# A two-layer graph attention on one core: where the exponential of h lies, how the rests of h are turned, and where the last aggregation's scores stand in the order

## The chip, the core and the metric

One core of a Trainium2 chip runs the whole kernel in one launch. The metric is the device time in microseconds (us), and the span is the part of it that the hardware profiler sees. Matmuls run on TensorE (PE; PEld are its weight loads), elementwise work on VectorE (DVE) and ScalarE (ACT), indirect gathers are issued on GpSimd (POOL), and most other transfers on SyncE (SP). Each engine takes its instructions in the order in which they were emitted; engines wait for one another by semaphores. SBUF is the memory on the chip, PSUM the one into which PE writes.

## The reference

3125 nodes with 768 features, 53125 edges (each node has a loop) sorted by target `dst`, three edge types. `x` goes through two layers of relational graph attention, then a residual sum and a layer norm:

```python
def rgat_conv(x, W, q, k, b, src, dst, etype, heads, out_ch, n_nodes):
    xr = jnp.einsum('nd,rdf->rnf', x, W)
    oi, oj = xr[etype, dst], xr[etype, src]
    alpha = jax.nn.leaky_relu(oi @ q + oj @ k, 0.2)
    m = jax.ops.segment_max(alpha, dst, num_segments=n_nodes)
    e = jnp.exp(alpha - m[dst])
    z = jax.ops.segment_sum(e, dst, num_segments=n_nodes)
    a = e / (z[dst] + 1e-16)
    msg = (a[:, :, None] * oj.reshape(-1, heads, out_ch)).reshape(-1, heads * out_ch)
    return jax.ops.segment_sum(msg, dst, num_segments=n_nodes) + b

h = jax.nn.elu(rgat_conv(x, W1, q1, k1, b1, ..., heads=4, out_ch=192))
out = rgat_conv(h, W2, q2, k2, b2, ..., heads=1, out_ch=768)
result = layernorm(x + out)          # over the 768 features, eps 1e-5
```

All inputs and outputs are float32.

## The kernel before, in words

The nodes are cut into `NB` = 25 blocks of 128. The edges of a block are fetched by gathers: each is one indirect DMA (L485, issued on POOL) of 128 rows of a table in device memory, 17 for a block (`SL`; 14 for block 0), 422 in all (`NK`) for each aggregation. The kernel has three stages.

The first (to some 520 us) multiplies x by W1 for the three edge types and stores the rows as the first table (`ftab`).

The second (some 520 to 1131 us, `phase2`, L844) aggregates over the first table and at once multiplies the result by W2, in the same order of blocks. For a block, in two halves of two heads' sums each: the rows are gathered; the scores are put together on DVE (`alpha`, L900 to L907), turned on PE (`turn`, into the PSUM tile `pa`), scanned for the maximum (`scan`, L921 to L926), taken through the exponential on ACT, turned back, and multiplied into selection matrices (`weigh`, L963); PE sums rows with them (`sums`, into `acc`). Then `e_y` (L1011) scales and adds the bias; `e_x` (L1023) takes the exponential on ACT; `e_h` (L1061) makes elu on DVE: L1063 min(ey,1)-1, L1065 for the last 64 of the 192 features of each head (the rests), L1066 for all. h is stored by four DMAs (`h_row`, L1068), and turned by PE (`e_t`, `turned`, L1034) by eight transposes into the two banks of `pt`: four of 128 features and four of the rests. `y` has 256 columns a head for this: 192 and a copy of the last 64. The turned h is split into a high part (`high_parts`: L1044 for the first bank, L1048 twice for the second, ACT) and a low part (`low_parts`: L1055, L1059 twice, DVE), so that products in reduced form add up to float32: `d_products` (L1091) does 72 matmuls a block against W2, in four pieces of 18. `d_row` (L1110) copies a piece's half row out of PSUM on ACT (L1117) and, after a row's second half, stores the whole row (L1119) into the second table. While blocks 15 to 24 are worked on, `move` (L1002 and the line after it) rewrites the table of row numbers piece by piece.

The third (1131 to 1725 us, `phase3`, L1185) gathers from the second table and sums in the same way, but with one head: `a_alpha` (L1305 to L1315), `a_turn`, `a_scan` (L1326 to L1331), `a_exp` (L1335), `a_back`, `weigh` (L1359), `sums` in eight rounds. The rows' own products are added as `r_plus` (L1420), and a product `D` with W2 follows: `d_part` (L1460), one matmul at a time, which the trace shows as two instructions, twelve parts for each block (36 for block 24, which uses W2 split into a high and a low part). That split is made by `w2_high` (L1427, six copies on ACT) and `w2_low` (L1431, six subtractions on DVE) in the buffers of gathers that are done by then. The residual sum and layer norm end a block (L1511 to L1550).

What sets the order is one list for each stage: steps are put down as `when(k, step, block, ...)`, where `k` is a number of slots (one slot per gather), the list is sorted by `k`, and the steps are emitted in that order. `STEPS2` (L89) and `STEPS3` (L103) hold the offsets of the steps from a block's first slot (second stage) or last slot (third). The third stage's scores stand at

```python
"s": (1.9, 3.0, 3.05, 3.1, 5.6, 5.7, 9.5),   # alpha, turn, scan, exp, back, weigh, sums
"d": ((19.5, 22.5, 7), (22.8, 26.2, 5)),      # twelve parts of the product
```

after the block's last slot (slot 422 for block 24), and the parts of the block before fall among them: with a distance of 17, two parts come before the turn and seven before the turn back. For all blocks, once, at the end (L1596):

```python
for t in range(DT):                            # DT = 6, NK = 422
    when(NK + 6 + 0.1 * t, w2_high, t)
    when(NK + 6.01 + 0.1 * t, w2_low, t)
```

Of the kernel before, what the change touches and what calls it, by code (L numbers as in the profile page):

```python
# [9 lines left out]
F32 = mybir.dt.float32  # L10
# [4 lines left out]
AF = mybir.ActivationFunctionType  # L15
ALU = mybir.AluOpType
# [5 lines left out]
P = 128  # L22
# [43 lines left out]
def _index(ap):  # L66
# [22 lines left out]
STEPS2 = {"first": (8.4, 9, 9.05, 11.3, 11.35, 17.4),  # L89
          "second": (16.35, 17.5, 17.55, 19.8, 19.85, 25.9),  # L90
          "f": (-4, 5),
          "marks": 3,
          "h": (26.1, 26.45, 28.4, 28.5, 34.52, 34.6, 34.62),
          "d": ((37, 38.5, 16), (43.2, 45.2, 20), (45.5, 47, 16), (51.7, 53.7, 20)),
          "second0": (13.3, 13.35, 13.4, 13.5, 13.6, 13.65),
          "sums0": (13.45, 13.55),
          "busy": ((0.3, 40), (9.02, 12)),
# [5 lines left out]
STEPS3 = {"f": -13,  # L103
          "marks": -5,
          "q": (-19, -17.27, -3.5, -2),
          "s": (1.9, 3.0, 3.05, 3.1, 5.6, 5.7, 9.5),
          "round": 0.9,
          "r": (16.7, 16.7, 16.72, 16.75, 19.25, 19.3, 16.71, 16.73, 20.5, 20.6),
          "t": (16.74, 16.78),
          "d": ((19.5, 22.5, 7), (22.8, 26.2, 5)),  # L110
          "y": (26.6, 26.7, 26.8, 29.5, 29.6),
# [4 lines left out]
def kernel(  # L116
# [21 lines left out]
    nc = tc.nc  # L138
# [3 lines left out]
    NB = (N + P - 1) // P  # L142
# [4 lines left out]
    H1 = l1["H"]  # L147
    F1 = D // H1
# [4 lines left out]
    HW = RW // 2  # L153
# [6 lines left out]
    V, S, G, T = nc.vector, nc.scalar, nc.gpsimd, Counted(nc.tensor)  # L160
# [14 lines left out]
    ident = keep.tile([P, P], F32, name="fident")  # L175
# [668 lines left out]
    def phase2(work, psum):  # L844
# [9 lines left out]
        rows = [work.tile([P, RW], F32, name=f"r2_{i}", bufs=1) for i in range(WHOLE)]  # L854
# [156 lines left out]
        def e_y(b):  # L1011
            s = blk[b]
            acc = [a[:, :HW].rearrange("p (w f) -> p w f", w=2) for a in s["acc"]]
            rz = work.tile([P, 2, 2], F32, name="rz", bufs=2)
            for c in range(2):
                V.tensor_scalar(rz[:, c], acc[c][:, :, F1], EPS, None, op0=ALU.add)
            V.reciprocal(rz, rz)
            y = s["y"] = work.tile([P, 4, 2 * P], F32, name="y", bufs=1)
            for w in range(4):
                V.scalar_tensor_tensor(y[:, w, :F1], acc[w // 2][:, w % 2, :F1], rz[:, w // 2, w % 2:w % 2 + 1],  # L1020
                                       bias1, op0=ALU.mult, op1=ALU.add)

        def e_x(b):  # L1023
            s = blk[b]
            s["ey"] = work.tile([P, 4, F1], F32, name="ey", bufs=1)
            S.activation(s["ey"], s["y"][:, :, :F1], AF.Exp)

        def busy(n):

# [3 lines left out]

        def turned(s, c):  # L1034

            for t in range(4):
                T.transpose(s["pt"][:, c, t * P:(t + 1) * P], s["y"][:, t, c * P:(c + 1) * P], ident)

        def high_parts(s, c):

            hT = s["hT"].rearrange("p s t (w i) -> p s t w i", i=32)
            pt = s["pt"][:, c].rearrange("p (w h i) -> p h w i", h=H1, i=32)
            if c == 0:
                S.copy(hT[:, 0, :H1], pt)  # L1044
                return
            for u in range(2):
                p = slice(64 * u, 64 * u + 64)
                S.copy(hT[p, 0, H1:], pt[p, u::2])  # L1048

        def low_parts(s, c):  # L1050

            hT = s["hT"].rearrange("p s t (w i) -> p s t w i", i=32)
            pt = s["pt"][:, c].rearrange("p (w h i) -> p h w i", h=H1, i=32)
            if c == 0:
                V.tensor_sub(hT[:, 1, :H1], pt, hT[:, 0, :H1].bitcast(F32))  # L1055
                return
            for u in range(2):
                p = slice(64 * u, 64 * u + 64)
                V.tensor_sub(hT[p, 1, H1:], pt[p, u::2], hT[p, 0, H1:].bitcast(F32))  # L1059

        def e_h(b):  # L1061
            s = blk[b]
            V.tensor_scalar(s["ey"], s["ey"], 1.0, -1.0, op0=ALU.min, op1=ALU.add)  # L1063
            y, ey = s["y"], s["ey"]
            V.scalar_tensor_tensor(y[:, :, F1:], y[:, :, P:F1], 0.0, ey[:, :, P:], op0=ALU.max, op1=ALU.add)  # L1065
            V.scalar_tensor_tensor(y[:, :, :F1], y[:, :, :F1], 0.0, ey, op0=ALU.max, op1=ALU.add)  # L1066

        def h_row(b):  # L1068

            s = blk[b]  # L1070
            s["rows"] = tab2[b * P * R:(b + 1) * P * R, :].rearrange("(n r) f -> n r f", r=R)
            to = s["rows"][:, WHOLE, :D].rearrange("(w i) (h f) -> h i w f", i=32, h=H1)
            for h in range(H1):
                nc.sync.dma_start(to[h], s["y"][32 * h:32 * h + 32, :, :F1])

        def e_t(b):
            s = blk[b]
# [34 lines left out]
        def d_row(b, p):  # L1112
            s = blk[b]
            po = s["po", p]
            r, c = divmod(p, 2)
            n = HW if c == 0 else D + 1 - HW
            S.copy(rows[r][:, c * HW:c * HW + n], po[:, :n])  # L1117
            if c == 1:
                nc.sync.dma_start(s["rows"][:, r, :], rows[r])  # L1119

        def d_tail(b, p):
# [13 lines left out]
        def when(k, f, *a):  # L1135
            ev.append((k, len(ev), f, a))
# [9 lines left out]
        for b in range(NB):  # L1146
            at_0 = base(b + 1) - SL
            when(max(at_0 + STEPS2["marks"], 0.5), marks, b)
            for u, name in enumerate(("first", "second")):
                when(max(at_0 + STEPS2["f"][u], 0.1 + 0.1 * u), f_load, b, u)  # L1150
                for d, f in zip(STEPS2[name], (alpha, turn, scan, back, weigh, sums)):
                    if b > 0:
                        when(at_0 + d, f, b, u)
                if b == 0:
                    for d, f in zip(STEPS2["second0" if u else name], (alpha, turn, scan, back, weigh, sums)):
                        if u == 1 or f is not sums:
                            when(d, f, b, u)
                    if u == 0:
                        for i, d in enumerate(STEPS2["sums0"]):
                            when(d, sums, b, u, i)  # L1160
            for d, f in zip(STEPS2["h"], (e_y, e_x, e_h, h_row, e_t, e_s, e_s2)):
                when(at_0 + d, f, b)
            n = 0
            for i, (a, e, m) in enumerate(STEPS2["d"]):
                for j in range(m):
                    when(at_0 + a + (e - a) * j / m, d_part, b)
                    n += 1
                    for p in range(4):
                        if n == 18 * (p + 1):
                            when(at_0 + a + (e - a) * j / m + STEPS2["copy"], d_row, b, p)  # L1170
                            when(at_0 + a + (e - a) * j / m + STEPS2["tail"], d_tail, b, p)
            assert n == 72
# [431 lines left out]
    with tc.manual_schedule():  # L1604
        with tc.tile_pool(name="share", bufs=1) as pool:
# [5 lines left out]
            with tc.tile_pool(name="wbuf", bufs=1) as wbuf:  # L1611
                weights[0] = [wbuf.tile([P, DT, WA], F32R, name=f"wa{s}") for s in "HL"]
                with tc.tile_pool(name="wrest", bufs=1) as wrest, tc.tile_pool(name="pre", bufs=1) as pre:
# [16 lines left out]
                    with tc.tile_pool(name="work0", bufs=1) as work, tc.tile_pool(  # L1630
                        name="psum0", bufs=1, space=PSUM
# [23 lines left out]
                    with tc.tile_pool(name="work1", bufs=1) as work, tc.tile_pool(  # L1655
                        name="psum1", bufs=1, space=PSUM
# [556 lines left out]
```

## Time and profile before

| | us |
|---|---|
| median of 3 runs | 1728.38 (1726.51 to 1731.38) |
| the profiled execution | 1726.83 |
| its span | 1724.9 |
| PE busy | 1640.5 (95%) |
| DVE busy | 1106.6 (64%) |
| POOL busy | 904.8 (52%) |
| ACT busy | 423.8 (25%) |
| DMA | 500.48 MB, mean 290 GB/s |

The span in 40 equal slices (43 us each); a digit is the busy share in tenths, for PEclk the granted clock of TensorE in tenths of 2.4 GHz:

```profile
PE   9999999999996999999999999939999999999996
POOL 5100000000007777777777777057777777777770
PEclk9999999999997999999999999969999999999999
DMA  9576766666568999999999999569999999999991
```

The two places where PE's digit falls (6 in the thirteenth slice, 3 in the twenty-seventh) are the changes of stage. POOL's digits show where gathers run. A busy share of 7 for POOL does not mean that it has time to spare: an indirect gather of 1.00 us is followed by 0.30 us that the profile counts as idle. The chain of waits follows the work that ended last back through what released it; a group of instructions has its mean duration in ns; a timeline lists the instructions of one engine in order of time.

### The profile page before, as it was taken

The page shows a single profiled execution, that of the slowest core. Times are in us where ns is not written, and L with a number is a line of the kernel's source. Part 1 is how long each engine was busy: PE and PEld are TensorE (multiplying, and loading weights), DVE is VectorE, ACT ScalarE, POOL GpSimd, SP SyncE. Part 2 cuts the span into 40 slices and gives each one's busy share as a digit, 9 for nine tenths or more (in the row PEclk, how much of TensorE's full clock was granted, in tenths as well). Part 3 has the DMA queues.
Part 4 walks back from the last instruction along what each step waited for, and adds up shares of the span by engine and source line. Part 5 has one row for each costly group of instructions (what it writes and reads, how often), then busy time and mean ns, then how long its engine had stood idle before and what let it go on. Part 6 is the DMA issues. An engine that isn't in the chain of part 4 may idle for free.

```text
span 1724.9 us, 39077 instructions
## 1 busy us (share of the span) xinstructions
PE 1640.5 (95%) x14233; PEld 1269.5 (74%) x14233; DVE 1106.6 (64%) x4107; ACT 423.8 (25%) x796; POOL 904.8 (52%) x907
## 2 busy tenths in 40 slices
PE   9999999999996999999999999939999999999996
PEld 8999999999995788888888888924444444444443
DVE  5467666676425566666677777465766666666665
ACT  5122222112110111111111111212333333333333
POOL 5100000000007777777777777057777777777770
PEclk9999999999997999999999999969999999999999
DMA  9576766666568999999999999569999999999991
GB/s 329 180 244 210 258 220 210 199 183 203 191 251 281 330 345 355 347 348 348 346 346 356 354 351 351 172 230 324 334 336 340 335 337 338 338 336 340 334 338 39
DMA packets 169368, 500.48 MB, mean 290 GB/s; under 512 B 39891, under 2 KB 82490, under 8 KB 169167
## 3 DMA queue, kind: packets, MB, share of 16 engines
q0 software_dynamic: 70832, 343.91, 56.1%
q1 hardware_dynamic: 90104, 143.89, 25.0%
q10 hardware_dynamic: 8230, 10.10, 1.7%
q8 instruction: 114, 1.87, 0.4%
q14 instruction: 88, 0.71, 0.1%
HBM read 412.96 MB, written 89.63 MB: 291 GB/s over the span
## 4 chain that ended last, share of the span: by engine, by line
PE 69%; DMA 12%; issue 8%; POOL 6%; DVE 4%; ACT 0%; POOLq 0%; DVEq 0%; ACTq 0%; SPq 0%
PE po L56 47%; PE acc L56 13%; PE D L56 4%; DMA waH<-ftab,ridx 3%; DMA waL<-ftab,ridx 3%; POOL waH L485 2%; PE pa L59 2%; PE pt L59 2%; DMA share<-ftab,ridx 1%; DMA extra<-ftab,ridx 1%; POOL waL L485 1%; POOL extra L485 1%; DMA spare_rows<-ftab,ridx 1%; POOL share L485 1%; PE bank L56 1%
## 5 line engine op out<-in xcount | busy, mean ns | idle before, releaser
L485 POOL DMA_INDIRECT extra<-ftab,ridx x296 | 303.3, 1025 | 90.2 <-issue 48.2
L56 PE MATMUL po<-waH,hT 128*128 128x386 f32 (+1 forms) x1200 | 323.1, 344 | 1.0 <-DVE hT L1055 0.8
L56 PE MATMUL po<-waH,xT 128*128 128x386 f32 x1104 | 293.0, 341 | 0.0
L485 POOL DMA_INDIRECT share<-ftab,ridx x209 | 214.2, 1025 | 63.7 <-issue 36.3
L56 PEld LDWEIGHTS po<-waH,hT 128*128 128x128 f32 x1200 | 220.4, 189 | 3.4 <-DVE hT L1055 1.1
L56 PE MATMUL po<-waL,hT 128*128 128x386 f32 (+1 forms) x600 | 207.6, 346 | 0.0
L56 PE MATMUL D<-extra,AT 128*128 128x512 f32 (+1 forms) x576 | 207.2, 503 | 0.0
L56 PEld LDWEIGHTS po<-waH,xT 128*128 128x128 f32 x1104 | 202.4, 189 | 0.5 <-issue 0.4
L56 PE MATMUL po<-waL,xT 128*128 128x386 f32 x552 | 186.9, 339 | 0.0
L598 ACT COPY share<-po 128x386 f32<-128x386 f32 x150 | 72.3, 482 | 371.2 <-PE po L56 298.7
L56 PEld LDWEIGHTS D<-extra,AT 128*128 128x128 f32 x576 | 105.6, 193 | 67.9 <-issue 60.3
L56 PE MATMUL acc<-waL,marks 128*32 128x386 f32 (+1 forms) x860 | 152.8, 490 | 0.0
L56 PE MATMUL po<-wbH,xT 128*128 128x386 f32 (+1 forms) x552 | 147.5, 341 | 1.3 <-DVE wbL L431 1.3
L56 PE MATMUL acc<-waH,marks 128*32 128x384 f32 (+1 forms) x828 | 141.3, 496 | 0.7 <-DVE marks L1359 0.7
L56 PE MATMUL acc<-extra,marks 128*32 128x386 f32 (+1 forms) x564 | 129.5, 487 | 0.0
L485 POOL DMA_INDIRECT waL<-ftab,ridx x108 | 108.1, 1001 | 32.9 <-issue 26.8
L56 PE MATMUL acc<-extra,sel 128*32 128x193 f32 x2736 | 122.6, 331 | 2.3 <-DVE sel L963 2.3
L927 ACT ACTIVATE e<-e 32x128 f32<-32x128 f32 (+2 forms) x50 | 15.5, 310 | 432.9 <-DVE e L926 432.9
L485 POOL DMA_INDIRECT waH<-ftab,ridx x103 | 102.8, 998 | 31.4 <-issue 25.0
L56 PEld LDWEIGHTS po<-waL,hT 128*128 128x128 f32 x600 | 113.7, 190 | 0.6 <-issue 0.3
L762 POOL DMA_DIRECT2D share<-in_L_gnn_W_dram x24 | 12.8, 536 | 188.4 <-DVE w2j L773 117.3
L56 PEld LDWEIGHTS acc<-extra,sel 128*32 128x32 f32 x2736 | 86.7, 111 | 31.4 <-issue 5.8
(312 smaller groups left out, 3078.1 us busy)
## 6 DMA issues: line engine op xcount, KB each, us to landing
ftab<-share SPq DMA_DIRECT2D x150, 193.0 KB
ftab<-r SPq DMA_DIRECT2D x50, 386.0 KB
sT<-dr_d SPq DMA_DIRECT2D x23, 544.0 KB
xb_d<-share SPq DMA_DIRECT2D x25, 384.0 KB
ftab<-y SPq DMA_DIRECT2D x100, 96.0 KB
share<-xb_d SPq DMA_DIRECT2D x25, 384.0 KB
share<-in_x_dram SPq DMA_DIRECT2D x24, 384.0 KB
out_dram<-share SPq DMA_DIRECT2D x24, 384.0 KB
```

The costliest lines, as they stand in the source:

```text
L56: return self.add(self.engine.matmul(to, weights, moving, **more), to, moving)
L59: return self.add(self.engine.transpose(to, a, unit), to, a)
L485: return G.indirect_dma_start(out=to, out_offset=None, in_=tab, in_offset=_index(i[:, j:j + 1]), bounds_check=NP * R - 1, oob_is_err=False)
L598: S.copy(o[:, :HW], po[:, :HW])
L762: G.dma_start(w2[i][p:p + n], l2["W"][r, at:at + n, :])
L927: S.activation(e, e, AF.Exp)
```

## The change

What it does, edit by edit:

- `y` is [128, 4, 192], the rests go into a tile `rest` [128, 256] of their own, and the exponential `ey` lies in PSUM (the tile `pt`) and no longer in SBUF. `e_h` reads it there.
- The rests are turned by two transposes of 128x128 (two heads at a time) and not four, so six in all. The copies out of the second bank become four of 64x128 (`rests`) on ACT and four on DVE; they were two of 64x256 on each.
- In the second stage's start: block 0's `e_t`, `e_s`, `e_s2` stand at 33.3 (34.52 before), block 1's first sums are split in two (30.25 and 31.4), and block 0's first 16 parts of the product stand at 34.6 to 36.1 (37 to 38.5).
- In the last block of the second stage, each half row is stored at once: four DMAs where two were.
- In the third stage the turn of the scores stands at 4.3 (3.0), scan 4.35, exponential 4.4, turn back 6.5 (5.6), weigh 6.6 (5.7), alpha 2.3 (1.9); the last `r_plus` at 21.37 (20.6). With the same places of the parts, five come before the turn and nine before the turn back.

```diff
@@ STEPS2
           "h": (26.1, 26.45, 28.4, 28.5, 34.52, 34.6, 34.62),
+          "h0": (26.1, 26.45, 28.4, 28.5, 33.3, 33.32, 33.34),
+          "sums1": (30.25, 31.4),
+          "d0": (34.6, 36.1, 16),
@@ STEPS3
-          "s": (1.9, 3.0, 3.05, 3.1, 5.6, 5.7, 9.5),
+          "s": (2.3, 4.3, 4.35, 4.4, 6.5, 6.6, 9.5),
           "round": 0.9,
-          "r": (16.7, 16.7, 16.72, 16.75, 19.25, 19.3, 16.71, 16.73, 20.5, 20.6),
+          "r": (16.7, 16.7, 16.72, 16.75, 19.25, 19.3, 16.71, 16.73, 20.5, 21.37),
@@ e_y, e_x
-            y = s["y"] = work.tile([P, 4, 2 * P], F32, name="y", bufs=1)
+            y = s["y"] = work.tile([P, 4, F1], F32, name="y", bufs=1)
+            s["rest"] = work.tile([P, 2 * P], F32, name="rest", bufs=1)
...
-            s["ey"] = work.tile([P, 4, F1], F32, name="ey", bufs=1)
-            S.activation(s["ey"], s["y"][:, :, :F1], AF.Exp)
+            ey = psum.tile([P, 2, 512], F32, name="pt", bufs=1)
+            s["ey"] = ey.rearrange("p c (w f) -> p (c w) f", w=2)[:, :, :F1]
+            S.activation(s["ey"], s["y"], AF.Exp)
@@ turned, rests, high_parts, low_parts
-            for t in range(4):
-                T.transpose(s["pt"][:, c, t * P:(t + 1) * P], s["y"][:, t, c * P:(c + 1) * P], ident)
+            if c == 0:
+                for t in range(4):
+                    T.transpose(s["pt"][:, 0, t * P:(t + 1) * P], s["y"][:, t, :P], ident)
+                return
+            for t in range(2):
+                T.transpose(s["pt"][:, 1, t * P:(t + 1) * P], s["rest"][:, t * P:(t + 1) * P], ident)
+        def rests(s, k):
+            hT = s["hT"].rearrange("p s t (m q i) -> p s t m q i", q=2, i=32)
+            pt = s["pt"][:, 1, :2 * P].rearrange("p (m t u i) -> p t m u i", m=2, u=2, i=32)
+            for u in range(2):
+                for q in range(2):
+                    yield hT[64 * u:64 * u + 64, k, H1:, :, q], pt[64 * q:64 * q + 64, :, :, u]
...
-            for u in range(2):
-                p = slice(64 * u, 64 * u + 64)
-                S.copy(hT[p, 0, H1:], pt[p, u::2])
+            for to, rest in rests(s, 0):
+                S.copy(to, rest)
...
-            for u in range(2):
-                p = slice(64 * u, 64 * u + 64)
-                V.tensor_sub(hT[p, 1, H1:], pt[p, u::2], hT[p, 0, H1:].bitcast(F32))
+            for (to, rest), (high, _) in zip(rests(s, 1), rests(s, 0)):
+                V.tensor_sub(to, rest, high.bitcast(F32))
@@ e_h
-            V.scalar_tensor_tensor(y[:, :, F1:], y[:, :, P:F1], 0.0, ey[:, :, P:], op0=ALU.max, op1=ALU.add)
-            V.scalar_tensor_tensor(y[:, :, :F1], y[:, :, :F1], 0.0, ey, op0=ALU.max, op1=ALU.add)
+            V.scalar_tensor_tensor(s["rest"].rearrange("p (w f) -> p w f", w=4), y[:, :, P:], 0.0, ey[:, :, P:], op0=ALU.max, op1=ALU.add)
+            V.scalar_tensor_tensor(y, y, 0.0, ey, op0=ALU.max, op1=ALU.add)
@@ d_row
-            if c == 1:
+            if b == NB - 1:
+                f = slice(c * HW, (c + 1) * HW)
+                nc.sync.dma_start(s["rows"][:, r, f], rows[r][:, f])
+            elif c == 1:
                 nc.sync.dma_start(s["rows"][:, r, :], rows[r])
@@ the second stage's order
+                    if b == 1 and u == 0 and f is sums:
+                        for i, d in enumerate(STEPS2["sums1"]):
+                            when(d, sums, b, u, i)
-                    if b > 0:
+                    elif b > 0:
                         when(at_0 + d, f, b, u)
...
-            for d, f in zip(STEPS2["h"], (e_y, e_x, e_h, h_row, e_t, e_s, e_s2)):
+            for d, f in zip(STEPS2["h" if b else "h0"], (e_y, e_x, e_h, h_row, e_t, e_s, e_s2)):
...
-            for i, (a, e, m) in enumerate(STEPS2["d"]):
+            for a, e, m in (STEPS2["d"] if b else (STEPS2["d0"],) + STEPS2["d"][1:]):
```

## Rows read from the trace of the kernel before

**Rows 1.** Windows, core 0: length, busy us (instructions) of each engine, granted clock, DMA share, GB/s
```profile
643.00:666.00 23.00, 23.00 (x273) 19.87 (x272) 15.14 (x49) 4.27 (x10) 17.66 (x18) 1.00 0.98 348
...
1600.40:1603.70 3.30, 3.25 (x6) 1.51 (x6) 3.01 (x9) 2.83 (x4) 2.39 (x4) 0.50 1.00 389
```

**Rows 2.** Chain of waits in the second stage: start us, us, what
```profile
818.42 0.87 PE pt L59 x8
...
841.20 0.87 PE pt L59 x8
...
848.79 4.38 PE acc L56 x104
```

**Rows 3.** Groups by line, POOL, third stage: busy us, mean ns, idle before, releasers
```profile
L485 POOL DMA_INDIRECT waH<-ftab,ridx x103 | 102.8, 998 | 31.4 <-issue 25.0 <-DMA waH<-ftab,ridx 1.8 <-DMA spare_rows<-ftab,ridx 0.9
```

**Rows 4.** Groups by line and shape, second stage, 800 to 1000 us
```profile
L1059 DVE TENSOR_TENSOR hT<-pt,hT 64x256 fp32r<-64x256 f32 x17 | 7.1, 417 | 0.1
...
L1048 ACT CAST hT<-pt 64x256 fp32r<-64x256 f32 x16 | 5.9, 366 | 0.1
...
L1063 DVE TENSOR_SCALAR ey<-ey 128x768 f32<-128x768 f32 x9 | 5.3, 591 | 0.0
...
L1044 ACT CAST hT<-pt 128x512 fp32r<-128x512 f32 x8 | 4.5, 566 | 0.0
```

**Rows 5.** Timeline of DVE, a usual block: start us, us, what [idle before, releaser]
```profile
837.02 0.96 DVE L1066 SCALAR_TENSOR_TENSOR y<-y,ey 128x768 f32<-128x768 f32 x1
...
839.09 0.18 DVE L907 COPY near<-al 64x28 f32<-64x28 f32 x1
...
845.85 2.02 DVE L963 TENSOR_TENSOR sel<-marks,pa 128x1152 f32<-128x1152 f32 x3
```

**Rows 6.** Timeline of DVE, a block with a table update
```profile
914.23 0.50 DVE L1002 TENSOR_SCALAR pall<-ridx,first_row,moved 128x425 f32<-128x425 int32 x1
...
915.40 2.02 DVE L963 TENSOR_TENSOR sel<-marks,pa 128x1152 f32<-128x1152 f32 x3
```

**Rows 7.** Timeline of PE, the same block's sums
```profile
917.12 2.17 PE L56 MATMUL acc<-share,sel 128*32 128x193 f32 x48
```

**Rows 8.** Groups by line and shape, whole span: DVE operations that read PSUM
```profile
L1420 DVE SCALAR_TENSOR_TENSOR share<-acc,half,share 128x768 f32<-128x768 f32 x50 | 50.3, 1007 | 1.7 <-ACT share L1415 0.8
...
L1511 DVE TENSOR_TENSOR share<-D,share 128x512 f32<-128x512 f32 x25 | 17.0, 682 | 0.7 <-PE D L56 0.7
```

**Rows 9.** Timeline of POOL, second stage
```profile
837.21 1.64 POOL L485 DMA_INDIRECT share<-ftab,ridx  x1 [0.30 <-DVE y L1065]
```

**Rows 10.** Chain of waits at the start of the second stage
```profile
594.38 7.15 DMA extra<-ftab,ridx
```

**Rows 11.** Chain of waits between the second stage and the third
```profile
1128.25 2.64 DMA ftab<-r
```

**Rows 12.** Chain of waits at the end
```profile
1687.81 3.87 PE D L56 x10
...
1691.84 2.35 PE D L56 x10
1694.20 10.50 PE acc L56 x120
```

**Rows 13.** Timeline of DVE at the end
```profile
1691.88 1.34 DVE L1359 TENSOR_TENSOR marks<-marks,pa 128x544 f32<-128x544 f32 x4 [0.48 <-PE pa L59]
1693.14 4.42 DVE L1431 TENSOR_TENSOR waH<-extra,waH 128x768 fp32r<-128x768 f32 x5
1697.49 0.95 DVE L1431 TENSOR_TENSOR waL<-extra,waH 128x768 fp32r<-128x768 f32 x1
```

**Rows 14.** Timeline of ACT at the end
```profile
1689.67 4.48 ACT L1427 CAST waH<-extra 128x768 fp32r<-128x768 f32 x6
```

**Rows 15.** Timeline of PE, third stage, around an idle time
```profile
1600.27 0.33 PE L59 MATMUL pa<-fident,al 128*17 128x128 f32 x1 [2.02 <-DVE al L1313]
...
1600.84 5.49 PE L56 MATMUL D<-extra,AT 128*128 128x512 f32 x10
```

More of the change, by code (lines that the diff above doesn't have):

```diff
@@ L1017, in e_y @@
             V.reciprocal(rz, rz)
-            y = s["y"] = work.tile([P, 4, 2 * P], F32, name="y", bufs=1)
+            y = s["y"] = work.tile([P, 4, F1], F32, name="y", bufs=1)
+            s["rest"] = work.tile([P, 2 * P], F32, name="rest", bufs=1)
             for w in range(4):
-                V.scalar_tensor_tensor(y[:, w, :F1], acc[w // 2][:, w % 2, :F1], rz[:, w // 2, w % 2:w % 2 + 1],
+                V.scalar_tensor_tensor(y[:, w], acc[w // 2][:, w % 2, :F1], rz[:, w // 2, w % 2:w % 2 + 1],
                                        bias1, op0=ALU.mult, op1=ALU.add)
@@ L1073, in h_row @@
             for h in range(H1):
-                nc.sync.dma_start(to[h], s["y"][32 * h:32 * h + 32, :, :F1])
+                nc.sync.dma_start(to[h], s["y"][32 * h:32 * h + 32])
         def e_t(b):
```

## The prediction

> **What bounds the kernel now.** I read the page's head first, then the chain of waits for who ends last, then windows and timelines in each stage. The profiled execution took 1726.83 us, 1.55 below the runs' median of 1728.38; its span is 1724.9, with 1.9 around it. All terms are sums against this execution; at the end I move them to the median.
>
> The second stage (520 to 1131 us: gather rows, weight and sum them, h, products with W2) is bound by TensorE. In a steady window PE is busy 23.00 of 23.00 us [rows 1], and the chain there is PE without a break: eight transposes into pt 0.87 us, sums 4.38, products between them; from pt to pt it is 22.8 us [rows 2]. POOL issues 17 gathers per block at 1.00 and a pause of 0.30, as in the third stage [rows 3], so 22.1: it is only 0.7 behind PE.
>
> The third stage (1131 to 1725) is bound by POOL's gathers: 103 of them take 102.8 us with 31.4 between [rows 3], 1.30 each and 22.15 per block. PE does 21.0 of work per block there and waits for each block's scores. So no reordering of PE's work shows in that stage before the last gather (1682.9): only the 42 us after it count.
>
> **The change part by part.**
>
> *Six transposes for eight.* 0.87 / 8 = 0.11 each [rows 2], so 0.22 less PE work per block. Over the 23 blocks after the start this is 5.0 if PE stays the bound. Neither POOL (0.7 below the period) nor the DMA queues (share 0.98 at 348 GB/s in that window, yet 389 elsewhere [rows 1]) stops at 0.22.
>
> *Four copies of 64x128 for two of 64x256, on ACT and on DVE.* No row has a 64x128. From below half the price (ACT 0.366 / 2, DVE 0.417 / 2 [rows 4]: nothing added); from above the full price each (+0.73 and +0.83). ACT's 366 ns for 256 columns against 566 for 512 gives 0.78 ns per column and 0.17 fixed; so 0.26 each, +0.3 on ACT. DVE's 417 for 256 against 682 for 512 (L1511 [rows 8]) gives 1.04 per column and 0.15 fixed; 0.28 each, +0.3. These stand in one chain (ACT's rests, DVE's first part, DVE's rests, weighing L963, sums). PE arrives 0.22 earlier too, so the chain loses 0.8 of its slack. In a usual block the first two of three weighing pieces run from 845.85 to about 847.5 [rows 5], the sums start at 848.79 [rows 2] and reach the second piece 0.17 later: slack 1.3, which hides it. In three blocks (sums near 917, 963 and 1008) a table update (L1002 and the line after it, 1.17 together) lies before the weighing, and L963 runs until 917.42 [rows 6] when the sums have started at 917.12 [rows 7]; the slack is 0.1 to 0.25. There 0.6 comes through: 3 x 0.6 = +1.8.
>
> *The exponential in PSUM.* L1063 takes 0.591 for 768 columns [rows 4]. For a DVE operation that reads PSUM, 682 ns for 512 columns (L1511) makes 682 + 256 x 1.04 = 948 for 768 by the slope above; L1420, 768 columns out of PSUM, has 1007 [rows 8]. That is the upper bound, no change the lower; I take 0.95 to 1.0, as both rows read PSUM. L1066 (0.96 [rows 5]) and L1065 stay near that. So +0.4 on DVE ahead of the scores. The scores' last piece (L907) ends at 839.27 [rows 5] and is turned 0.33 ahead of pt, at 840.87 [rows 2]: usual slack 1.5; in the blocks with a table update it is 0.05 to 0.9, so some +0.5 in all (0 to 2).
> The Trainium skill ("VectorE: DVE Perf Modes", section "Mode 2×_2P") says that a one-source fp32 operation reaches two results per cycle only with source and destination in SBUF. The trace agrees that L1063 is faster per column than L1511, 0.77 against 1.33 ns [rows 4, 8]; the rule speaks against this edit with the same +0.4.
> In the SBUF form, L1066 (837.02, 0.96) lies beside a gather of 1.64 instead of 1.00 [rows 5, 9]. The Trainium skill ("SBUF — State Buffer", section "SBUF: two separate sides") says that a DVE operation with two SBUF inputs keeps GpSimd off the port they share for its whole length. By that rule POOL would gain 0.6 per block; as PE is the bound there, the sum would not change.
>
> Second stage, net: -5.0 + 1.8 + 0.5 = **-2.7** (-5 to -0.5).
>
> *First h amid the next sums.* Before the steady part PE waits for gathers landing: the longest such piece of the chain is 7.15 us from 594.38 [rows 10]. Work moved earlier by about 2 us waits for the same landings. Only unstretched gathers of the first two blocks may give something: **-0.6** (-1 to +0.3).
>
> *Half-row stores in the last block.* The third stage's first gather waits for the store of the last row: 2.64 of DMA from 1128.25 [rows 11]. With the first half already sent, the last store is half as large, but its packets too, and there are two issues on SP. Bounds 0 and -1.3 (half of 2.64), and +0.3 for the extra issue; I take **-0.4**, near "no change", since most of such a short store is not transfer.
>
> *Scores behind five parts; scales behind nine; weigh at 6.6; last addition at 21.37.* In blocks 1 to 23 POOL hides it (1.15 of slack per block). After the last gather the scores of block 24 are still turned near 1687.5, since the turn before it stays tied to its gathers; but three fewer parts follow it. Of the ten parts that now stand between turn and sums (3.87 + 2.35 [rows 12]) seven remain, some 2 us less: the last sums would start at 1692.1 instead of 1694.20. But the steps w2_high and w2_low (six ACT copies, six DVE subtractions for the last block's split product) stand at slots 428.0 to 428.51 of the order. The last weighing stood at 422 + 5.7 = 427.7, ahead of them; it now stands at 422 + 6.6 = 428.6, behind all six on DVE. Its new place: the exponential ends about 1689.7; one L1420 (1.01 [rows 8]) then runs to some 1690.6; the first w2_high is done by then too (six take 4.48 from 1689.67 [rows 14]); six L1431 in a row take from 1693.14 to 1698.44 = 5.3 [rows 13], so to 1695.9; the weighing 1.34 [rows 13], to 1697.2. The sums read the last weighed piece in their first round, so they start at 1697.4 where they did at 1694.2: +3.2.
> PE then idles over 5 us. After an idle of 2.02 [rows 15] the granted clock was 0.50 for 1600.4 to 1603.7 [rows 1] (the 1.2 GHz level), and the ten matmuls there took 5.49 [rows 15] instead of the 3.87 that ten take here [rows 12]: +1.6. Whether the clock falls again is open (0 to 2.0); the idle is twice as long, so I take +1.6: 3.2 + 1.6 = **tail +4.8** (+2.5 to +6.5). What is cheaper later, w2_low done early, buys nothing: nothing waited for it before.
>
> Sum: -0.6 - 2.7 - 0.4 + 4.8 = +1.1. 1726.83 + 1.1 = 1727.9; against the median, 1728.38 + 1.1 = **1729.5**.
>
> **The rivals.**
>
> *B, faster.* The second stage gains its full 5.0 (blocks with table updates find the time), the start and the store another 2.2, and the last weighing costs little: w2_low meets PE work that is still left and the clock stays at 1.00, tail +0. For it: the steady chain has no gap [rows 2]. Against it: seven parts last under 5 us and the six subtractions alone 5.3 [rows 13]. 1728.4 - 7.2 = 1721.2.
>
> *C, slower.* One mechanism: the copies cost by instruction, not by column. Then ACT gets +0.73 and DVE +0.83, with 0.22 from PE 1.78 against a slack of 1.33: sums wait 0.45 in every block, decided from 1.1 of added copy time. 24 x (0.45 - 0.22) = +5.5 for -2.7, the rest as forecast: 1729.5 + 8.2 = 1737.7. For it: ACT has 366 ns at 256 and not half of 566, so a fixed part is there [rows 4]. Against it: that fixed part is 0.17, under half.
>
> *D, the change doesn't do what it says.* The second stage is paced by gathers' DMA (share 0.98 [rows 1]), and the shorter PE work just waits: -2.7 becomes 0 to +0.5, 1732.5. Against it: PE busy 23.00 of 23.00.
>
> **How the numbers follow.** Forecast 0.61, own range 1725 to 1734; B 0.17; C 0.12; D 0.10. A measurement of this kernel tells 0.3% from no change, which is 5.2 us: faster is below 1723.2, slower above 1733.6. Faster: B nearly whole and a little of the forecast, 0.19. Slower: C whole, a third of D and a twelfth of the forecast, 0.20. Within: 0.61. The range leaves out the far halves of B and C: 1722.5 to 1735.5.
>
> **What would show it.** Second stage right: period pt to pt 22.5 to 22.6, six transposes in 0.65, and sums waiting for L963 only near 917, 963, 1008. Wrong: PE waits for L963 in every block (C), or the period stays at 22.8 with PE waiting for gathers (D). L1063 at 0.9 to 1.0. Tail right: six L1431 ahead of the last four L1359 on DVE, PE idle some 5 us before the last sums, a granted clock of 0.50 behind it, and over 42 us from the last gather to the end (some 46 to 48). The prediction fails if that idle stays under 2 us, or if the first two stages move more than 6 us.

## The result, and the profile after

The changed kernel takes 1732.95 us (median of 9 runs, 1730.76 to 1738.96), the kernel before 1727.43 in the same sets (9 runs, 1725.63 to 1731.38): a ratio of 1.0031, 95% interval 1.0019 to 1.0043. It is 5.5 us slower; 1729.5 was forecast, in a range to 1735.5.

The profiled execution has a span of 1729.2 for 1724.9. The page after: busy us, share and instructions of each engine.

```profile
span 1729.2 us, 39073 instructions
...
PE 1637.2 (95%) x14183; PEld 1341.6 (78%) x14183; DVE 1125.3 (65%) x4157; ACT 429.6 (25%) x846; POOL 895.3 (52%) x907
```

PE has 3.3 us less work than before.

Four stretches account for the 4.3 us between the two spans (one execution of each kernel), each measured between the same two events in both traces. Second stage, from its first gather to the transposes of block 3: 116.36 before, 118.96 after, **+2.6**. From there to the last product: 491.65 and 490.00, **-1.65**. From there to the end of the last gather: 555.18 and 553.53, -1.65 (0.94 of it between the last product and the third stage's first gather, 0.7 in the gathers behind). From the end of the last gather to the end: 42.07 and 47.00, **+4.9**. The first stage differs by 0.05.

**Second stage, steady part.** The chain of waits (start us, us, what), where [rows 2] stood:

```profile
819.41 0.66 PE pt L59 x6
...
841.96 0.66 PE pt L59 x6
```

Six transposes take 0.66 for 0.87, and the period (from one block's transposes to the next block's) is 22.55 to 22.61 for 22.75 to 22.82. The new and changed operations by line and shape (busy us, mean ns, idle before):

```profile
L1074 DVE TENSOR_TENSOR hT<-pt,hT 64x128 fp32r<-64x128 f32 x36 | 10.3, 286 | 0.4
...
L1064 ACT CAST hT<-pt 64x128 fp32r<-64x128 f32 x34 | 8.8, 259 | 0.3
L1078 DVE TENSOR_SCALAR pt<-pt 128x768 f32<-128x768 f32 x9 | 8.6, 958 | 0.0
```

The short copies cost 286 ns on DVE (L1074, 0.28 expected) and 259 on ACT (L1064, 0.26); the exponential's first step out of PSUM 958 for the 591 of [rows 4] (0.95 to 1.0 expected). This agrees with what the Trainium skill says in "VectorE: DVE Perf Modes", section "Mode 2×_2P": a one-source fp32 operation does two results a cycle only where source and destination lie in SBUF.

**Second stage, blocks 16, 18, 20 and 22.** Their periods are 23.75, 23.36, 23.27 and 22.99, together 3.0 above the usual; before, only block 16 was longer, with 22.94. The chain around the first of them, two pieces of it:

```profile
914.71 0.30 DVE hT L1074
915.04 0.51 DVE pall L1005
915.58 0.60 DVE pall L1006
916.22 1.36 DVE sel L966
917.62 4.55 PE acc L56 x104
...
926.93 4.86 DMA share<-ftab,ridx
...
932.84 0.29 DVE near L910
```

Low parts on DVE (L1074), a table update (L1005, L1006) and the weighing L966 stand in one line here, and PE's sums (917.62) wait for the end of it; the usual block has no update in that place. In the second piece the scores begin at 931.81. The chain names a landing, which ended at 931.79; on DVE another table update ends at the same time, as its timeline shows:

```profile
931.29 0.60 DVE L1006 TENSOR_TENSOR pall<-pall 128x425 f32<-128x425 f32 x1
```

DVE has no idle time from 922.54 up to these scores, so this trace can't tell which of the two held them.

**The start.** POOL's timeline (start us, us, what, idle before and its releaser):

```profile
559.37 1.00 POOL L488 DMA_INDIRECT share<-ftab,rfirst  x1 [0.30 <-issue]
563.33 1.00 POOL L488 DMA_INDIRECT share<-ftab,rfirst  x1 [2.96 <-PE pt L59]
```

The first gather of block 2 stands 2.96 us behind the one before it, where every other pause is 0.30; the releaser is PE's transposes of block 0. In the chain the price comes later, as landings that PE waits for:

```profile
577.65 5.78 DMA extra<-ftab,rfirst
...
584.16 6.59 DMA share<-ftab,rfirst
```

**Between the stages.** The store that the third stage's first gather waits for ([rows 11]):

```profile
1129.25 1.88 DMA ftab<-r
```

1.88 for 2.64. From the last product to the first gather it is 3.22 for 4.16.

**The end.** The chain after the last gather (ended 1682.21), where [rows 12, 13] stood:

```profile
1681.73 0.53 PE D L59 x3
...
1682.98 4.40 PE D L56 x10
...
1690.31 4.43 DVE waH L1452 x5
1694.74 0.87 DVE waL L1452
1695.61 0.64 DVE marks L1380
...
1696.29 12.23 PE acc L56 x120
```

Two windows of it (length, busy us of PE, PEld, DVE, ACT and POOL, granted clock, DMA share, GB/s):

```profile
1690.00:1696.00 6.00, 1.41 (x6) 0.91 (x6) 5.83 (x8) 5.22 (x7) 0.00 (x0) 0.97 0.00 0
1696.30:1699.00 2.70, 2.70 (x17) 1.62 (x21) 2.63 (x8) 0.00 (x0) 0.00 (x0) 0.50 0.00 0
```

The six subtractions L1452 run before the last weighing L1380, PE idles in between (busy 1.41 of 6.00, a pause of 4.88), and the sums then run at a granted clock of 0.50 until 1699. The sums start 14.08 behind the last gather for 11.34 (+2.7), take 12.23 for 10.50 (+1.7), and what follows takes 0.5 more.

The last gather is a loose mark, though, since PE isn't tied to it here. The chain of the kernel before shows PE's own order, with the rest of it in [rows 12]:

```profile
1684.51 0.53 PE D L59 x3
...
1685.77 1.82 PE D L56 x4
```

From the turn of block 23's sums (D L59) to the last sums it is 9.69 before and 14.56 after: 4.9 more, the whole pause. This turn stood 1.65 behind the last gather before and 0.48 ahead of it after, so in this one execution some 2.1 us of the loss don't show in the +4.9. Five other kernels below have the same end (e1, e2, e4, e5, e7). In their traces the pause is 4.88 again, the sums take 12.2 to 13.2, and from the last gather to the end it is 48.0 to 48.6.

### The profile page after: what moved, and what is told of

The parts are those of the page before. It is cut to its first block, busy times and chain, and to the rows that moved or that the text cites. A ratio compares the mean times of both kernels' runs of the same rounds, so it can differ in the third digit from the quotient of the medians.

```text
span 1729.2 us, 39073 instructions
## 1 busy us (share of the span) xinstructions
PE 1637.2 (95%) x14183; PEld 1341.6 (78%) x14183; DVE 1125.3 (65%) x4157; ACT 429.6 (25%) x846; POOL 895.3 (52%) x907
## 4 chain that ended last, share of the span: by engine, by line
PE 66%; DMA 11%; issue 8%; DVE 8%; POOL 6%; ACT 1%; POOLq 0%; DVEq 0%; ACTq 0%; SPq 0%
PE po L56 45%; PE acc L56 15%; DMA waH<-ftab,ridx 3%; PE D L56 2%; DMA waL<-ftab,ridx 2%; DMA share<-ftab,ridx 2%; DMA extra<-ftab,ridx 2%; POOL extra L488 2%; POOL waH L488 2%; PE pa L59 2%; POOL waL L488 1%; PE pt L59 1%; DVE share L1441 1%; POOL share L488 1%; PE bank L56 1%
## 5 line engine op out<-in xcount | busy, mean ns | idle before, releaser
L488 POOL DMA_INDIRECT extra<-ftab,ridx x296 | 297.9, 1006 | 93.5 <-issue 48.8
L488 POOL DMA_INDIRECT share<-ftab,ridx x209 | 210.5, 1007 | 67.2 <-issue 32.6
L56 PE MATMUL D<-extra,AT 128*128 128x512 f32 (+1 forms) x576 | 202.6, 494 | 0.0
L488 POOL DMA_INDIRECT waH<-ftab,ridx x103 | 103.0, 1000 | 31.4 <-issue 25.6
```

The source lines that it names most:

```text
L56: return self.add(self.engine.matmul(to, weights, moving, **more), to, moving)
L488: return G.indirect_dma_start(out=to, out_offset=None, in_=tab, in_offset=_index(i[:, j:j + 1]), bounds_check=NP * R - 1, oob_is_err=False)
```

## Experiments

Twelve kernels ran. Ratios are to the kernel before, in the same set; the changed kernel stands at 1.0031.

| kernel | edit to the changed kernel | median us | ratio (95%) |
|---|---|---|---|
| e1 | old start of the second stage | 1729.36 | 1.0009 (0.9997 to 1.0022) |
| e2 | block 2's gathers not paced | 1727.89 | 1.0003 (0.9991 to 1.0014) |
| e3 | W2's split behind the last weighing | 1725.99 | 0.9994 (0.9980 to 1.0007) |
| e4 | exponential in SBUF | 1732.46 | 1.0021 (1.0008 to 1.0033) |
| e5 | table updates at fixed places | 1727.99 | 1.0003 (0.9994 to 1.0013) |
| e6 | third stage's old order of scores | 1727.35 | 1.0004 (0.9992 to 1.0016) |
| e7 | last rows stored whole | 1734.31 | 1.0043 (1.0028 to 1.0057) |
| e8 | e2, e3 and e5 together | 1718.23 | 0.9944 (0.9927 to 0.9961) |
| e12 | kernel before with e2's and e5's edits | 1727.81 | 1.0002 (0.9992 to 1.0011) |

e9, e10 and e11 ran where the kernel before itself took 1980 us; they are told at the end of this section.

**e1, e2: what holds the gather at the start.** Each gather from block 2 on has an added wait on an instruction of PE ("the gathers keep the pace of the products"). Which instruction is found by counting PE's work between the places of two blocks' first gathers in the list of steps. The new start moves work of PE across the place of block 2.

```diff
-for d, f in zip(STEPS2["h" if b else "h0"], ...)   # e1: "h", "d" for all blocks,
+for d, f in zip(STEPS2["h"], ...)                  #     block 1's first sums in one
...
-            paced(i, 2, b, j, -5.5)                # e2
+            paced(i, 2, b, j, -5.5, b != 2)
```

> The changed kernel with the old start of the second stage (block 0's h, block 1's first sums and block 0's first product parts in their old places); all else as changed. Theory (the new order makes the first gather of block 2 wait for a later instruction of PE, so POOL stands still for 2.96 us at 560.4): that idle time falls back to 0.30, the transposes of block 1 come near 589 where they came at 592.01 (589.03 before), and the time falls by 2.5 to 3 us against the changed kernel, to about 1.0015 of the kernel before. Rival (the start waits for landings in either order, and the 3 us come from the dearer copies of h): transposes of block 1 at 591 or later, time within 1 us of the changed kernel, 1.003 of before.

> The changed kernel with its new start, but the gathers of block 2 no longer keep pace with PE (line 878's wait left out for that block alone; buffers still guard themselves). Theory (the pacing wait alone holds POOL at 560.4): the idle of 2.96 us falls to 0.30, the transposes of block 1 come at 589 to 590 and the time falls by 2 to 3 us against the changed kernel. Rival (the gather waits for its buffer, which block 1's split sums free later): the idle stays over 2 us and the time stays within 0.7 us of the changed kernel.

POOL's timeline of e1:

```profile
559.95 1.00 POOL L488 DMA_INDIRECT share<-ftab,rfirst  x1 [0.30 <-issue]
561.25 0.99 POOL L488 DMA_INDIRECT share<-ftab,rfirst  x1 [0.30 <-issue]
```

And of e2:

```profile
559.58 1.00 POOL L488 DMA_INDIRECT share<-ftab,rfirst  x1 [0.30 <-issue]
560.88 1.00 POOL L488 DMA_INDIRECT share<-ftab,rfirst  x1 [0.30 <-issue]
```

In both the pause is 0.30 again. e2 keeps the new start and its split sums, so neither these nor the buffers held the gather: the pacing wait did. From the first gather to the transposes of block 3 it is 115.47 in e1 and 114.49 in e2 (118.96 changed, 116.36 before). So in the new start the pacing wait costs 4.5: the six traces with both have 118.1 to 119.6 there, the two without the wait (e2, e8) 114.5 and 114.6. The times agree: 0.0028 of 1728 is 4.8 us for e2, 0.0022 or 3.8 for e1, both more than the 2 to 3 expected. That the new start is faster than the old one is not shown. e2 is 1.0 ahead of e1, but e12 below, with the old start and without the wait, has 114.76. e1's transposes of block 1 came at 590.75, not near 589, but its stage began 0.7 later.

**e3: what holds the last sums.**

```diff
-            when(NK + 6 + 0.1 * t, w2_high, t)
-            when(NK + 6.01 + 0.1 * t, w2_low, t)
+            when(NK + 6.7 + 0.1 * t, w2_high, t)
+            when(NK + 6.71 + 0.1 * t, w2_low, t)
```

> The changed kernel with the six w2_high and six w2_low at slots NK + 6.7 and on, behind the last weighing (NK + 6.6). Theory (the last sums wait for the weighing behind the six subtractions, and the idle lowers PE's clock): last sums start at 1692 to 1693 where they started at 1696.29, PE idle before them under 1 us (5.28), granted clock 1.00 behind them (0.50 for 1696.3 to 1699), time 4.5 to 5.5 us less than the changed kernel, 1.000 of the kernel before. Rival (the split of W2 then comes too late for the last product, which is as long a wait): the sums start early, but a wait of 3 us or more stands ahead of the last product, and the time falls by less than 2 us.

The chain of e3 (last gather ended 1686.74):

```profile
1687.46 0.55 PE D L59 x3
...
1688.74 4.40 PE D L56 x10
...
1693.36 2.15 PE D L56 x8
...
1695.68 1.49 PE D L56 x6
1697.17 10.57 PE acc L56 x120
...
1709.60 0.57 DVE waL L1478
1710.21 6.58 PE D L56 x36
```

A window of e3, columns as above:

```profile
1696.00:1699.00 3.00, 3.00 (x30) 1.98 (x32) 3.00 (x7) 3.00 (x6) 0.00 (x0) 1.00 0.00 0
```

The sums follow the product's parts without a gap, the clock stays at 1.00, and no wait for W2's split stands ahead of the last product (1709.60, the low part of the turned sums, then 1710.21). From last gather to end it is 41.6 for 47.0, and the time falls by 0.0037, 6.4 us; 4.5 to 5.5 were expected. The pause (4.9) and the slower sums (1.7) make 6.6. The sums start 10.4 behind the last gather (14.08 changed); in the changed kernel's time that is 1692.6, as expected.

e3 also shows what the new order is worth there. From the turn of block 23's sums to the last sums it is 9.71, where the kernel before has 9.69. The product's twelve parts, two instructions each, all stand between them in both kernels: 10 + 8 + 6 here, 4 + 10 + 10 before. The new order puts three parts ahead of the turn of the scores and no longer behind it; PE has no idle time there and comes to the sums as late as before. So behind the last gather the new order gains nothing by itself.

**e4: the exponential in SBUF again.**

```diff
-            ey = psum.tile([P, 2, 512], F32, name="pt", bufs=1)
-            s["ey"] = ey.rearrange("p c (w f) -> p (c w) f", w=2)[:, :, :F1]
+            s["ey"] = work.tile([P, 4, F1], F32, name="ey", bufs=1)
```

> The changed kernel with the exponential of h in a tile of SBUF again; six transposes and eight short copies stay. Theory (PSUM costs DVE 0.37 us a block, which shows only where a table update stands close; the stretched gathers cost nothing while PE is the bound): L1078 back from 0.958 to about 0.59, one gather a block stretched to about 1.6 again, period pt to pt still 22.57, the steps over 23 us at blocks 16, 18, 20 and 22 (23.75, 23.36, 23.27, 22.99) smaller by 0.2 to 0.4 each, time 0 to 2 us less than the changed kernel. Rival (the stretched gathers hold the stage at the shorter period, so the PSUM form is what lets PE gain): period back to 22.7 to 22.8 with PE waiting for gathers, time 2 to 4 us more than the changed kernel.

The first operation of e_h in e4, by line and shape:

```profile
L1077 DVE TENSOR_SCALAR ey<-ey 128x768 f32<-128x768 f32 x9 | 5.0, 553 | 0.0
```

POOL's timeline of e4, the gathers beside e_h:

```profile
836.12 1.26 POOL L488 DMA_INDIRECT share<-ftab,ridx  x1 [0.30 <-issue]
837.68 1.15 POOL L488 DMA_INDIRECT share<-ftab,ridx  x1 [0.31 <-issue]
```

The period stays at 22.57, and the long ones are 23.38, 23.24, 23.24 and 22.56: 0.95 less in all. Two gathers of a block are stretched by 0.41 together, not one by 0.6. Gathers are busy some 17.4 of a block here and 17.1 in the changed kernel. The Trainium skill ("SBUF — State Buffer", section "SBUF: two separate sides") has a DVE operation with two SBUF inputs keep GpSimd out of the port that they share for its whole length. The rows agree in that gathers beside e_h take longer, by 0.26 and 0.15; a stretch of the operation's whole length they don't show. With its pauses of 0.30 POOL then needs some 22.5 of the 22.57, so it has next to nothing to spare, yet PE isn't kept waiting and the rival falls: nothing is lost by the SBUF form here. Whether the PSUM form costs 1 to 2 us is not settled by the times, as the intervals overlap.

**e5: table updates out of the way.**

```diff
-            when(base(late) + STEPS2["move"] + i * (NB - 1 - late) * SL / (NB - 2), move, i + 1)
+            when(base(late + 1 + i // 3) + (8.7, 17.0, 17.6)[i % 3] - SL, move, i + 1)
```

> The changed kernel with the 24 table updates (L1005, L1006) of blocks 15 to 22 at three fixed places in a block, where DVE waits for PE or ACT anyway (slots 8.7, 17.0 and 17.6: behind the scores' first and second part, and ahead of the low parts); before, they stood every 6.65 slots and so at another place in each block. Theory (only the blocks where an update stands between the rests and the weighing, or between e_h and the scores, lose time): the four long periods 23.75, 23.36, 23.27 and 22.99 (blocks 16, 18, 20, 22) fall to about 22.57, and the time by 2.5 to 3.3 us against the changed kernel, to about 1.0015 of the kernel before. Rival (gathers or the pace of POOL, late by then, make those stalls): periods stay over 22.9 in at least three of these blocks, time within 1 us of the changed kernel.

DVE's timeline of e5 (the first of the two operations of an update, and what follows):

```profile
922.23 0.68 DVE L924 TENSOR_TENSOR_SCAN F<-f,pa 32x256 f32<-32x256 f32 x1 [1.33 <-PE pa L59]
...
934.18 0.49 DVE L1005 TENSOR_SCALAR pall<-ridx,first_row,moved 128x425 f32<-128x425 int32 x1
...
936.14 0.69 DVE L1071 TENSOR_TENSOR hT<-pt,hT 128x512 fp32r<-128x512 f32 x1 [0.83 <-ACT hT L1064]
```

The updates fill time in which DVE waits for PE (1.33 of it left at 922.23) or ACT (0.83 left at 936.14, where it was 1.88). All periods from block 4 to 23 are 22.55 to 22.60, and the time falls by 0.0028, 4.8 us, more than the 3.0 that the four periods add up to. The rival falls.

**e6 and e7: the old order of the scores; whole rows stored.**

```diff
-          "s": (2.3, 4.3, 4.35, 4.4, 6.5, 6.6, 9.5),     # e6, and the last addition at 20.6
+          "s": (1.9, 3.0, 3.05, 3.1, 5.6, 5.7, 9.5),
...
-            if b == NB - 1:                                # e7
-                f = slice(c * HW, (c + 1) * HW)
-                nc.sync.dma_start(s["rows"][:, r, f], rows[r][:, f])
-            elif c == 1:
+            if c == 1:
```

> The changed kernel with the third stage's old order of scores (turn at 3.0, back 5.6, weigh 5.7, last addition 20.6). Theory (the new order costs 5 us behind the last gather, nothing before it): from the end of the last gather to the end of the span 41.5 to 42.5 us (47.0 changed, 42.1 before), no idle of 5 us ahead of the last sums, time 4 to 5 us less than the changed kernel, 1.0005 of before. Compared with w2 moved behind the weighing it tells what the new order is worth by itself: 0 to 2 us. Rival (the order also helps blocks 1 to 23): the last gather ends 1 us or more later and the gain stays under 3 us.

> The changed kernel with the last block's rows stored whole again (two DMAs for four). Theory: the store that the first gather of the third stage waits for takes 2.6 us for 1.88, the first gather comes 0.7 to 1.0 later behind the last product, time 0.5 to 1.0 us more than the changed kernel, within what a measurement tells. Rival (the distance is set by POOL's own start, not by the store): less than 0.3 us.

e6's time falls by 0.0027, 4.7 us, as expected. Its one profiled execution shows less (45.1 behind the last gather, not 41.5 to 42.5): the sums have no gap ahead of them, but the last turn comes 7.0 behind its gather for 4.6 before. One block earlier PE had waited 1.72 for scores, and the granted clock was lower behind it. Two windows of e6, columns as above:

```profile
1666.50:1669.00 2.50, 2.22 (x5) 0.99 (x5) 2.37 (x7) 1.97 (x2) 1.89 (x3) 0.63 1.00 403
1669.00:1672.50 3.50, 3.50 (x8) 1.44 (x6) 1.68 (x2) 1.84 (x3) 2.59 (x4) 0.77 1.02 367
```

So where the last turn falls behind its gather varies by 2 us between executions, and one trace can't weigh edits of that size by the distance from the last gather. The rival, that the new order helps blocks 1 to 23, holds in small part: from the third stage's first gather to the end of its last it is 550.8 to 551.0 in the three traces with the old order (before, e6, e12) and 549.8 to 550.5 in the eight with the new one.

In e7 the chain from the last product on:

```profile
1129.71 3.15 DMA f<-ed_d
...
1132.87 0.40 POOL waH L488
```

The chain names the short load `f` that was issued behind the store (L1134); the kernel before has the same load as the releaser of that gather in POOL's timeline. From last product to first gather 4.10 (3.22 changed, 4.16 before): the half stores give 0.9. By time it is 0.0012, 2 us, with intervals that overlap.

**e8 and e12: all three mends, and the control.**

> The changed kernel with three mends at once: block 2's gathers not paced, w2's split behind the last weighing, table updates at fixed places. Theory (the three losses are apart in time and add): 4.5 + 5.5 + 3 = 13 us less than the changed kernel if all come through, near 1720 (0.996 of before); at least 9 us less. Rival (the losses overlap, since POOL's gathers then bind the second stage): 6 us less or under, PE waiting for gathers in the second stage, period over 22.7.

> The same kernel as e11_before_mended (the kernel before with table updates at fixed places and block 2's gathers not paced), once more, since that set ran where gathers bound every stage (kernel before 1980 us). Where the kernel before takes about 1727: theory (its pacing wait doesn't bind, and its only long period is 22.94 at block 16): 0 to 1 us less than before, ratio 0.9994 to 1.0005, steady period 22.8, so that most of e8_three's 0.9944 is the change's own once three of its losses are mended. Rival (the mends gain by themselves): ratio under 0.998.

The sum of the three gains is 0.0028 + 0.0037 + 0.0028 = 0.0093; e8 has 0.0087 (15 us) less than the changed kernel. The losses were apart and add. It is 8.7 us faster than the kernel before. e12 gives the kernel before two of the mends (the third it has by its order) and moves by 0.0002: its steady period is 22.8, and its long ones are gone too, but it had only one of 22.94. So the two mends gain nothing without the change, and what e8 gains is the change's own.

Its trace, of the slowest of its five runs, tells where in part. The span is 5.8 less than the one before. From block 3 to the last product it is 487.80 (491.65 before, 491.47 in e12), about 0.2 in each period. From there to the first gather it is 3.35 for 4.16, and the third stage's gathers take 1.2 less. The start has 114.60, but e12 has 114.76, so no gain of the new start is shown. The end has none: the last sums start at 1688.25, right behind the product's parts, and from the last gather to the end it is 43.5 for 42.1 before.

**e9, e10, e11: no answer to their questions.** They ran on another chip, where the kernel before took 1980.48 (1975.83 to 1989.21). PE there is busy 186 of 200 us in the second stage, and DMA moves 293 GB/s where it moved 349. The window 800 to 1000 us of e11, columns as above:

```profile
800.00:1000.00 200.00, 186.14 (x1967) 153.41 (x1967) 112.38 (x355) 32.35 (x76) 126.15 (x125) 1.00 0.90 293
```

And of the kernel before, in its own trace:

```profile
800.00:1000.00 200.00, 200.00 (x2393) 172.26 (x2396) 148.31 (x460) 36.61 (x85) 154.64 (x149) 1.00 0.98 349
```

> The kernel with the three mends (e8_three) and the exponential of h in SBUF again. Theory (PSUM form costs DVE time that a block has to spare once the table updates are out of the way; the stretched gathers cost nothing, since POOL at 22.3 a block is still ahead of PE's 22.57): period 22.57, time within 1.2 us of e8_three (1718.23). Rival 1 (stretched gathers now bind): period over 22.65 or waits of PE for gathers, 2 us or more slower. Rival 2 (the PSUM form still costs): 1.5 us or more faster.

> The kernel with the first and third mend (no pace in block 2, table updates at fixed places) and, in place of the moved w2 split, the third stage's old order of scores. Against e8_three it tells what the new order is worth once the w2 split no longer stands in its way. Theory (three parts of the product less stand between the last scores and the last sums): 1.5 to 2 us slower than e8_three. Rival (the last scores themselves come later by as much, since the product's parts now stand ahead of them): within 0.7 us.

> The kernel before with the first and third mend alone (its w2 split is already behind the weighing). Theory (before, neither the pacing wait nor the table updates cost more than a few tenths: blocks 16 at 22.94 is the only long period): 0 to 1 us less than the kernel before, so the 8.7 us of e8_three are the change's own. Rival (the mends gain by themselves): 3 us or more less than before.

Ratios there: e9 1.0005 (0.9990 to 1.0021), e10 1.0016 (0.9996 to 1.0035), e11 1.0031 (1.0012 to 1.0049). PE there stands idle for 14 of 200 us; that gathers land more slowly than it works is likely, but the chain names no releaser for most of its waits. On this chip no kernel is faster than the one before, and the two mends of e11 lose 6 us. So the times don't tell what the new order of scores is worth by itself (the traces: nothing behind the last gather, about 1 us or less ahead of it), and whether the PSUM form is worth keeping in e8 stays open. (e11's kernel is that of e12.)

## Why the prediction held, and where it did not

*Six transposes, short copies, exponential in PSUM.* The prices were right: 0.21 off the period, 259 and 286 ns, 958 ns. PE stayed the bound, so rivals C and D are out.

*Table updates.* Forecast: three blocks, 1.8 + 0.5 us. Measured: four, 3.0 in all. In the first three of the long periods the sums start 0.60, 0.64 and 0.62 late, as forecast. e4 tells the two terms apart: with the exponential in SBUF those three keep 2.1 above the usual and the fourth is gone. So the weighing cost 2.1 for 1.8, and the scores behind the longer exponential 0.95 for 0.5, the larger error. e5 confirms that the updates are the cause.

*First h amid the next sums.* This step failed: "Work moved earlier by about 2 us waits for the same landings", -0.6, where it was +2.6. I took the landings as given, while the gathers carry a wait on PE's own order of instructions (one line in the gather step that I left out of the account). Moving PE's steps moved the instruction waited for; 2.96 us of POOL standing still, 3.5 us in the end against the old start (e1). Without that wait the step nearly holds: 114.60 in e8 with the new start, 114.76 in e12 with the old. It was a wait on POOL's queue, in the code and not in any row of the trace before, because there it never came last.

*Half stores.* -0.4 forecast, -0.94 in the trace.

*Scores behind five parts.* Forecast +4.8 behind the last gather, measured +4.9. The mechanism was right: the six subtractions ahead of the weighing, a pause (over 5 forecast, 4.88 measured) and the clock behind it (+1.6 and +1.7). e3 shows both the place and the price. But that the sum came out at +4.9 was luck. One step of it failed, "the turn before it stays tied to its gathers; but three fewer parts follow it". The turn comes when PE has done the parts ahead of it, which take 4.40 for 1.82, so the 2 us taken off for the three parts aren't there. The turn came near 1687.5 all the same, because PE was 2.1 us earlier against the last gather in that one execution. The loss itself is 6.6, as e3's time says (6.4), and the five other traces with this end have +5.9 to +6.5.

The sum was +1.1 where the trace has +4.3 and the medians 5.5. In the trace it was 3.2 too low at the start of the second stage and 1.0 too low in its steady part; the half stores gave 0.5 more than forecast, and 0.7 in the third stage's gathers was not forecast. Rival B had the right size for a kernel without these losses (1721.2; e8 has 1718.23), with the wrong reason.

## What to carry to other kernels

Before a step is moved in an in-order queue, list everything keyed to a place in that order: waits by count or by cycle, and steps with fixed slots (W2's split) that the moved step now falls behind. A saving on the bounding engine becomes a stall wherever a rare piece of work stands in the chain that just lost slack; put where its engine waits anyway, that piece cost nothing here. Putting work ahead of a step and not behind it gains nothing on an engine without idle time. Three separate losses of 15 us together hid a gain of 8.7, and each was confirmed by an edit of its own.

## What the hardware showed that was not expected

The same program is 15% slower on one chip (1980 for 1727 us). For the kernel of e11 and e12, DMA moves 293 GB/s there and 349 elsewhere in the window 800 to 1000 us, at busy shares of 0.90 and 0.97. How kernels compare changes with the chip (that kernel against the one before: 1.0031 there, 1.0002 here). And a pause of PE of 1.72 us was followed by a granted clock of 0.63 and 0.77 in the two windows after it (e6), one of 2.02 [rows 15] by 0.50, while one of 2.34 in the kernel before, up to 1489.4, was followed by 1.00 up to 1492.8. The pause of 4.88 cost 1.7 us in the sums behind it, and 1.5 to 2.6 in the five other traces that have it.
